# Expert loop of a hybrid block: biases in a tile of their own, token numbers copied apart, another place for the small tiles, and sums read three tokens a partition

## The chip, the cores and the metric

The kernel runs on one core of a Trainium2 chip. The metric is the time of one execution on the device, in microseconds (us); the time of a kernel is the median of several executions. The core has five engines that work side by side and wait for each other through semaphores: TensorE (PE; the load of its weights is listed apart as PEld), VectorE (DVE), ScalarE (ACT), GpSimd (POOL) and SyncE (SP). Transfers are issued from queues of SyncE, ScalarE and GpSimd (SPq, ACTq, POOLq) and carried out by 16 DMA engines. A profile is one execution taken by the hardware profiler.

## What is computed

An image of 2 x 256 x 48 x 48 goes through two layers: a convolution and attention layer, then a state-space layer with a mixture of experts on 2 x 2304 = 4608 tokens of 256 channels. The change concerns the last stage alone, the mixture of experts, and the writing of the result:

```python
def _L1_ffn_ref(x, Wg, bg, W1, b1, W2, b2):            # 8 experts, 256 -> 1024 -> 256
    gate_logits = xf @ Wg + bg
    top_w, top_i = jax.lax.top_k(gate_logits, 2)        # each token goes to two experts
    top_w = jax.nn.softmax(top_w, axis=-1)
    w_dense = jnp.sum(jax.nn.one_hot(top_i, E) * top_w[..., None], axis=1)
    for e in range(E):
        h = jax.nn.gelu(xf @ W1[e] + b1[e], approximate=False)
        out = out + w_dense[:, e:e + 1] * (h @ W2[e] + b2[e])
# ...
t = t + _L1_ffn_ref(_ln_t(t), ...)
x = _from_tokens(t, x)                                  # tokens x channels -> channels x tokens
```

## The kernel before

Before the expert stage every token has been written twice into a table in HBM (`xs`), once for each of its two experts, so that the rows of one expert stand together. A row has 256 channels, 8 gate weights and the number of the token (`XW` = 265 words). The residual stream stands in `acc`, one row of 256 channels a token. The expert stage works through 40 tiles: 36 of 256 rows ("pairs", the 2 in `tiles`) and 4 of 128 rows (the 1). Which rows and which expert a tile has is computed on the chip (`plan`). A branch for four more tiles of 128 rows stands behind the loop and is not taken here.

```python
every = NPAIR // (NUSUAL + 1)                     # 36 // 5 = 7: a 128-row tile after 7, 14, 21, 28 pairs
for i in range(NPAIR):
    tiles.append((2, i))
    if i % every == every - 1 and i // every < NUSUAL:
        tiles.append((1, i // every))
# ...
def fetch(i):                                     # rows and weights of tile i, issued by SyncE
    halves, n = tiles[i]
    x = hp.tile([P, 2, XW], F32, tag="ex", name="ex", bufs=4)[:, :halves]
    # ... (tile 0 apart)
    row = self.value(at[0:1, 0, n : n + 1], sp, NROWS - TR)
    part = self.value(at[0:1, 1, n : n + 1], sp, (E - 1) * P)
    nc.sync.dma_start(x, self.expert_rows(self.xs[bass.ds(row, halves * P), :]))
    wt = ew.tile([P, WCOL], F32, tag="wt", name="wt")               # 3 buffers: W1, W2, b1, b2, one-hot of the expert
    self.tc.keep_in_program_order(nc.sync.dma_start(wt, ins["We"][bass.ds(part, P), :]))
    fetched[i] = x, wt

def turn(i):                                      # rows transposed to ext; the gate weight of each row
    x, wt = fetched[i]
    xt = hp.tile([P, NH, halves * P], F32, tag="ext", name="ext")
    self.transposes(xt..., [x[:, j, k * P : (k + 1) * P] for k in range(NH) for j in range(halves)], nc.vector.tensor_copy)
    own = hp.tile([P, halves, E], F32, tag="own", name="own")
    nc.vector.tensor_tensor(own, x[:, :, C : C + E], bcast(wt[:, WCOL - E :], 1, [P, halves, E]), ALU.mult)
    weight = hp.tile([P, halves], F32, tag="weight", name="weight")
    nc.vector.tensor_reduce(weight, own, AX.X, ALU.add)

def weight_sums(i):                               # pairs: four sums of blocks of W2 (ts), VectorE
    # ... t1 = b12 - b11; t3 = b22 - b12; t2 = b22 - t1; t4 = b21 - t2
def hidden_sums(i):                               # pairs: four sums of blocks of hid (ss), VectorE
    # ... s3 = a11 - a21; s1 = a21 + a22; s2 = s1 - a11; s4 = a12 - s2

def up(i):                                        # hid = gelu(x W1 + b1)
    for c in range(NHC):                          # 8 times
        ps = self.bank()                          # 4 banks
        # ... two matmuls
        nc.scalar.activation(hid[:, c, :], ps[:, :rows], AF.Gelu, bias=b1[:, c : c + 1])

def finish(i, y, j):                              # weighted, and added to acc by an accumulating indirect DMA
    x, weight = fetched[i][0], turned[i][1]
    nc.scalar.activation(y, y, AF.Identity, scale=weight[:, j : j + 1])
    token = x[:, j, XW - 1 :].bitcast(I32)
    put = nc.gpsimd.indirect_dma_start(self.acc, bass.IndirectOffsetOnAxis(ap=token, axis=0), y, None, compute_op=ALU.add)
    # ... the two stores of one tile have no order between them; those of different tiles have

def down(i):                                      # y = hid W2 + b2
    # 128 rows: 8 matmuls, y = po + b2, finish
    # pairs: Strassen-Winograd's seven products of half size, four matmuls each, in the order
    #   a11 b11, s3 t3, a12 b21, a22 t4, s1 t1, s2 t2, s4 b22
    nc.scalar.copy(p1, p[1])
    # ... seven additions on VectorE make y0 and y1
    for j, y in enumerate((y0, y1)):
        add(y, y, b2)                             # b2 lies in wt
        finish(i, y, j)

def run(first, end):
    for i in range(first, end):
        up(i)
        if i + 1 < end: turn(i + 1)
        if tiles[i][0] == 2: hidden_sums(i)
        down(i)
        if i + 1 < end: weight_sums(i + 1)
        if i + 3 < end: fetch(i + 3)
# ...
for g in range(B * NBLK):                         # at the end: 12 blocks of 384 tokens of acc are read
    # ... a partition gets three tokens that lie 128 apart
    (nc.sync, nc.scalar)[g % 2].dma_start(t, self.acc[g * TB : (g + 1) * TB, :].rearrange("(j p) c -> p j c", p=P))
for g, t in enumerate(blocks):                    # transposed and written
    for k in range(NH):
        o = hp.tile([P, TB], F32, tag="o", name="o", bufs=6)
        self.transposes(o, [t[:, j, k * P : (k + 1) * P] for j in range(NJ)], nc.vector.tensor_copy)
        (nc.sync, nc.scalar)[k].dma_start(self.out[b, k * P : (k + 1) * P, blk * TB : (blk + 1) * TB], o)
```

The order of the instructions on each engine isn't that of this text: a scheduler moves instructions whose inputs are there ahead of others. In the loop `own` of a tile stands up to two tiles ahead of its place.

Of the kernel before, what the change touches and what calls it, by code (L numbers as in the profile page):

```python
# [31 lines left out]
F32 = mybir.dt.float32  # L32
I32 = mybir.dt.int32
AF = mybir.ActivationFunctionType
ALU = mybir.AluOpType
AX = mybir.AxisListType

P = 128
B, C, H, W = 2, 256, 48, 48
N = H * W  # L40
NH = C // P
# [23 lines left out]
NJ = 3  # L65
TB = NJ * P
NBLK = N // TB
# [3 lines left out]
E, HID = 8, 1024  # L71
NHC = HID // P
# [4 lines left out]
NPAIR, NSINGLE = 2 * B * N // TR, E  # L77
NUSUAL = E // 2
NROWS = E * PART + TR
XW = C + E + 1  # L80
WCOL = NH * HID + NHC * C + NHC + C + E
F32_EPS = float(np.finfo(np.float32).eps)


# [30 lines left out]
def bcast(ap, axis, shape):  # L115
    return ap.unsqueeze(axis).to_broadcast(shape)
# [108 lines left out]
class Kernel:  # L225
# [1496 lines left out]
    def experts(self, ctx):  # L1722
        nc, ins = self.nc, self.ins
        self.psum(ctx, 4, 2)
        hp = self.pool("eh", 2, ctx)
        ew = self.pool("ew", 3, ctx)
# [4 lines left out]
        fetched, turned, hidden, sums = {}, {}, {}, {}  # L1731

        tiles = []
        every = NPAIR // (NUSUAL + 1)
        for i in range(NPAIR):
            tiles.append((2, i))
            if i % every == every - 1 and i // every < NUSUAL:
                tiles.append((1, i // every))
        usual = len(tiles)
        tiles += [(1, i) for i in range(NUSUAL, NSINGLE)]  # L1740
# [10 lines left out]

        def fetch(i):
            halves, n = tiles[i]
            x = hp.tile([P, 2, XW], F32, tag="ex", name="ex", bufs=4)[:, :halves]
            if i == 0:
                self.tc.keep_in_program_order(nc.sync.dma_start(x, self.expert_rows(self.xs[0:TR, :])))
                fetched[i] = x, self.first_weights
                return
            at = where[2 - halves]
            row = self.value(at[0:1, 0, n : n + 1], sp, NROWS - TR)  # L1760
            part = self.value(at[0:1, 1, n : n + 1], sp, (E - 1) * P)
            nc.sync.dma_start(x, self.expert_rows(self.xs[bass.ds(row, halves * P), :]))
            wt = ew.tile([P, WCOL], F32, tag="wt", name="wt")
            self.tc.keep_in_program_order(nc.sync.dma_start(wt, ins["We"][bass.ds(part, P), :]))
            fetched[i] = x, wt

        def turn(i):

            halves = tiles[i][0]
            x, wt = fetched[i]  # L1770
            xt = hp.tile([P, NH, halves * P], F32, tag="ext", name="ext")
            self.transposes(
                xt.rearrange("p k q -> p (k q)"),
                [x[:, j, k * P : (k + 1) * P] for k in range(NH) for j in range(halves)], nc.vector.tensor_copy,
            )
            own = hp.tile([P, halves, E], F32, tag="own", name="own")
            nc.vector.tensor_tensor(  # L1777
                own, x[:, :, C : C + E], bcast(wt[:, WCOL - E :], 1, [P, halves, E]), ALU.mult
            )
            weight = hp.tile([P, halves], F32, tag="weight", name="weight")  # L1780
            nc.vector.tensor_reduce(weight, own, AX.X, ALU.add)
            turned[i] = xt, weight

        def weight_sums(i):

# [24 lines left out]

        def up(i):
            rows = tiles[i][0] * P
            xt, wt = turned[i][0], fetched[i][1]
            w1 = wt[:, : NH * HID].rearrange("p (k o) -> p k o", k=NH)
            b1 = wt[:, WCOL - C - NHC - E : WCOL - C - E]
            hid = hidden[i] = hp.tile([P, NHC, rows], F32, tag="hid", name="hid")
            for c in range(NHC):
                ps = self.bank()
                for k in range(NH):
                    nc.tensor.matmul(  # L1820
                        ps[:, :rows], lhsT=w1[:, k, c * P : (c + 1) * P], rhs=xt[:, k, :],
                        start=k == 0, stop=k == NH - 1,
                    )
                nc.scalar.activation(hid[:, c, :], ps[:, :rows], AF.Gelu, bias=b1[:, c : c + 1])  # L1824

        def finish(i, y, j):

            x, weight = fetched[i][0], turned[i][1]
            nc.scalar.activation(y, y, AF.Identity, scale=weight[:, j : j + 1])  # L1829
            token = x[:, j, XW - 1 :].bitcast(I32)  # L1830
            put = nc.gpsimd.indirect_dma_start(  # L1831
                self.acc, bass.IndirectOffsetOnAxis(ap=token, axis=0), y, None, compute_op=ALU.add
            )
            self.tc.declare_no_dep(put.ins, group=f"tile{i}", reason="a token has one row of an expert")
            self.tc.add_to_no_dep_group(f"tile{i}", put.ins)

        def down(i):
            wt, hid = fetched[i][1], hidden[i]
            w2 = wt[:, NH * HID : NH * HID + NHC * C].rearrange("p (k o) -> p k o", k=NHC)
            b2 = wt[:, WCOL - C - E : WCOL - E]  # L1840
            banks = self.ps2.tile([P, 2, 512], F32, tag="banks", name="po")
            if tiles[i][0] == 1:
                y = hp.tile([P, C], F32, tag="ey", name="ey", bufs=5)
                po = banks[:, 0, :C]
                for c in range(NHC):
                    nc.tensor.matmul(po, lhsT=hid[:, c, :P], rhs=w2[:, c, :], start=c == 0, stop=c == NHC - 1)
                nc.vector.tensor_add(y, po, b2)
                finish(i, y, 0)
            else:
                v = sums.pop(i)  # L1850
                p = {}

                for n, (name, a, w) in enumerate((
                    (1, "a11", "b11"), (7, "s3", "t3"), (2, "a12", "b21"), (4, "a22", "t4"), (5, "s1", "t1"),
                    (6, "s2", "t2"), (3, "s4", "b22"),
                )):
                    p[name] = banks[:, n // 4, n % 4 * P : (n % 4 + 1) * P]
                    for c in range(NHC // 2):
                        nc.tensor.matmul(p[name], lhsT=v[a][:, c], rhs=v[w][:, c], start=c == 0, stop=c == NHC // 2 - 1)  # L1859
                y0, y1 = (hp.tile([P, C], F32, tag="ey", name="ey", bufs=5) for _ in range(2))  # L1860
                p1, u2, u3, u4 = (hp.tile([P, P], F32, tag=f"u{j}", name=f"u{j}", bufs=1) for j in range(4))
                add = nc.vector.tensor_add
                nc.scalar.copy(p1, p[1])  # L1863
                add(y0[:, :P], p[2], p1)
                add(u2, p[6], p1)
                add(u3, p[7], u2)
                add(u4, p[5], u2)
                add(y1[:, :P], p[4], u3)
                add(y1[:, P:], p[5], u3)
                add(y0[:, P:], p[3], u4)  # L1870
                for j, y in enumerate((y0, y1)):
                    add(y, y, b2)
                    finish(i, y, j)
            del fetched[i], turned[i], hidden[i]
# [26 lines left out]
        with self.tc.If(self.value(many[0:1, 0:1], list(self.nc.engines), NSINGLE) > NUSUAL):  # L1901
# [2 lines left out]
            turn(usual)  # L1904
            run(usual, len(tiles))

        blocks = []
        for g in range(B * NBLK):
            b, blk = divmod(g, NBLK)
            t = self.x[b].rearrange("p k n -> p (k n)")[:, blk * NJ * C : (blk + 1) * NJ * C]  # L1910
            t = t.rearrange("p (j c) -> p j c", j=NJ)
            (nc.sync, nc.scalar)[g % 2].dma_start(
                t, self.acc[g * TB : (g + 1) * TB, :].rearrange("(j p) c -> p j c", p=P)
            )
            blocks.append(t)
        for g, t in enumerate(blocks):
            b, blk = divmod(g, NBLK)
            for k in range(NH):
                o = hp.tile([P, TB], F32, tag="o", name="o", bufs=6)
                self.transposes(o, [t[:, j, k * P : (k + 1) * P] for j in range(NJ)], nc.vector.tensor_copy)  # L1920
                (nc.sync, nc.scalar)[k].dma_start(self.out[b, k * P : (k + 1) * P, blk * TB : (blk + 1) * TB], o)

    def run(self):
        nc = self.nc
# [4 lines left out]
        for b in range(B):  # L1929
            for i in range(NX):  # L1930
                part = slice(i * N // NX, (i + 1) * N // NX)
# [25 lines left out]
        nc.vector.tensor_copy(self.taken, self.c["base"])  # L1957
        self.first_weights = self.pool("ew0", 1).tile([P, WCOL], F32, name="wt")
        nc.sync.dma_start(self.first_weights, self.ins["We"][0:P, :])
        with ExitStack() as l1:  # L1960
            self.mamba(l1)
        with ExitStack() as ffn:
            self.experts(ffn)


@with_exitstack
# [30 lines left out]
def _arrays(i):  # L1997
# [29 lines left out]
        "W_in": w_in, "W_out": at("W_out").T,  # L2027
        "We": experts.reshape(E * P, WCOL),
        "vec": np.concatenate([vec[k] for k in _VEC], axis=1),
# [21 lines left out]
```

## Time and profile before

| | |
|---|---|
| time | 1411.49 us, median of 3 (1408.32 to 1415.42) |
| span of the profile | 1414.2 us |
| TensorE busy | 1269.9 us, 90% |
| VectorE busy | 1013.5 us, 72% |
| ScalarE busy | 780.4 us, 55% |
| GpSimd busy | 531.3 us, 38% |
| the expert loop on TensorE | 838.4 to 1374.2 us, mean clock 0.99, 203 GB/s |
| from its end to the first read of the sums | 1374.2 to 1383.1 us |
| reading, transposing, writing | 1383.1 to 1414.2 us, 304 GB/s |

How to read lines of the profile. A line of the timeline gives the start and the length in us, the engine, the line of the kernel, the operation, what it writes and reads, how often, and in brackets how long the engine stood idle before it and what ended that. A line of the chain of work that ended last gives start, length and what it was. A line of the waits says who waited for whom, for how many us in all, how many times, and the longest. A stretch of the windows gives its length, the busy time of PE, PEld, DVE, ACT and POOL, the granted clock of TensorE as a share of full speed, the busy share of the DMA engines, and GB/s. `acc<-ey,ex` is the accumulating store of `finish`.

### The profile page before, as it was taken

How to read it: one execution, taken by the hardware profiler on the slowest of the kernel's cores; microseconds unless marked ns; L12 is line 12 of the kernel's file. 1: busy time of each engine (PE TensorE's matmuls, PEld its weight loads, DVE VectorE, ACT ScalarE, POOL GpSimd, SP SyncE). 2: the span in 40 equal slices, each digit the busy share in tenths (PEclk: the TensorE clock that was granted, in tenths of full speed). 3: DMA queues.
4: the chain of work that ended last, by engine and by line, in shares of the span. 5: the costliest groups of instructions: out<-in, count | busy, mean ns of one | idle time of the engine just before them, and what ended most of it. 6: DMA issues, size and time to landing. Idle time of an engine off the chain costs nothing.

```text
span 1414.2 us, 23686 instructions
## 1 busy us (share of the span) xinstructions
PE 1269.9 (90%) x8144; PEld 1012.9 (72%) x8144; DVE 1013.5 (72%) x2610; ACT 780.4 (55%) x1920; POOL 531.3 (38%) x648
## 2 busy tenths in 40 slices
PE   5999999998998899999988539998999999999983
PEld 4566767666666566666665429997998999998983
DVE  4999999997788889899978636654645645655653
ACT  2688877897987777777866212332332332432320
POOL 5213030111466777778676831221222222221220
PEclk9999999997999999999999859999999999999996
DMA  7321413121332233324243147666566667666628
GB/s 285 107 88 46 138 38 105 37 64 65 116 99 82 68 90 107 101 93 120 82 127 100 57 134 279 209 194 214 177 217 225 180 218 232 196 208 219 203 50 275
DMA packets 100442, 199.54 MB, mean 141 GB/s; under 512 B 10059, under 2 KB 86044, under 8 KB 94876
## 3 DMA queue, kind: packets, MB, share of 16 engines
q1 hardware_dynamic: 80540, 171.57, 36.4%
q0 software_dynamic: 14400, 19.74, 6.6%
q10 hardware_dynamic: 5380, 6.69, 1.4%
q8 instruction: 66, 1.08, 0.3%
q14 instruction: 56, 0.46, 0.1%
HBM read 158.71 MB, written 44.18 MB: 143 GB/s over the span
## 4 chain that ended last, share of the span: by engine, by line
PE 38%; DVE 15%; DMA 14%; ACT 3%; issue 3%; POOL 2%; another core or an unknown queue 0%; SPq 0%; DVEq 0%; ACTq 0%; POOLq 0%
PE bank L1820 11%; PE po L1859 10%; DMA wt<-in_We 7%; DMA acc<-ey,ex 5%; PE bank L909 4%; PE zbank L909 3%; PE bank L1420 2%; DVE xc L1106 2%; PE bank L895 1%; PE bank L1359 1%; PE bank L1402 1%; DVE mt L1322 1%; ACT mt L1314 1%; DVE y L1410 1%; POOL xs L1629 1%
## 5 line engine op out<-in xcount | busy, mean ns | idle before, releaser
L1820 PE MATMUL bank<-ext,wt 128*128 128x256 f32 (+1 forms) x1280 | 275.5, 373 | 10.0 <-ACT hid L1824 9.2
L1831 POOL DMA_INDIRECT acc<-ey,ex x76 | 118.5, 1559 | 435.0 <-ACT ey L1829 394.8
L1820 PEld LDWEIGHTS bank<-ext,wt 128*128 128x128 f32 x1280 | 233.0, 192 | 41.7 <-ACT hid L1824 11.7
L1824 ACT ACTIVATE hid<-bank,wt 128x256 f32<-128x256 f32 (+1 forms) x320 | 143.0, 462 | 83.0 <-PE bank L1820 79.0
L1863 ACT COPY u<-po 128x128 f32<-128x128 f32 x36 | 9.6, 266 | 226.6 <-PE po L1859 226.6
L1859 PE MATMUL po<-ts,ss 128*128 128x128 f32 x864 | 108.4, 275 | 0.0
L1859 PEld LDWEIGHTS po<-ts,ss 128*128 128x128 f32 x864 | 102.6, 192 | 0.0
L585 DVE SCALAR_TENSOR_TENSOR x<-hid,w2r,x 128x1128 f32<-128x1128 f32 (+3 forms) x72 | 99.9, 1392 | 0.4 <-ACT hid L579 0.2
L909 PE MATMUL bank<-xn,win 128*128 128x387 f32 x240 | 94.3, 517 | 1.1 <-DVE lg L1445 1.0
L1777 DVE TENSOR_TENSOR own<-ex,wt 128x16 f32<-128x16 f32 (+1 forms) x40 | 6.9, 173 | 122.9 <-DMA wt<-in_We 114.8
L674 POOL COPY kp<-kp 128x10 f32<-128x10 f32 (+1 forms) x60 | 23.4, 390 | 190.2 <-DVE kp L667 190.2
L793 ACT ACTIVATE prob<-prob,top 128x308 f32<-128x308 f32 x144 | 78.2, 549 | 17.4 <-DVE top L782 17.0
L1314 ACT ACTIVATE mt<-mt,cum 128x128 f32<-128x128 f32 x288 | 87.4, 392 | 0.0
L1106 DVE SCALAR_TENSOR_TENSOR xc<-bank,vec,xc 128x384 f32<-128x384 f32 x144 | 85.1, 605 | 2.4 <-ACT xc L1095 2.2
L909 PE MATMUL zbank<-xn,win 128*128 128x384 f32 x192 | 77.6, 529 | 4.2 <-ACT z L1216 4.2
L1629 POOL DMA_INDIRECT xs<-u,rows x72 | 71.9, 999 | 22.5 <-issue 16.7
L1859 PE MATMUL po<-wt,hid 128*128 128x128 f32 x576 | 77.5, 278 | 0.0
L1420 PE MATMUL bank<-wout,y 128*128 128x264 f32 x288 | 72.9, 398 | 2.6 <-DVE ss L1435 1.3
L1859 PEld LDWEIGHTS po<-wt,hid 128*128 128x128 f32 x576 | 71.7, 195 | 0.1
L824 PE MATMUL bank<-pt,val 110*64 110x128 f32 (+1 forms) x864 | 69.4, 278 | 0.8 <-ACT pt L814 0.8
L799 ACT ACTIVATE prob<-prob,rden 128x308 f32<-128x308 f32 x144 | 67.7, 547 | 4.3 <-DVE rden L848 4.2
L824 PEld LDWEIGHTS bank<-pt,val 110*64 110x64 f32 (+1 forms) x864 | 58.7, 136 | 14.7 <-issue 10.2
(288 smaller groups left out, 2982.7 us busy)
## 6 DMA issues: line engine op xcount, KB each, us to landing
wt<-in_We SPq DMA_DIRECT2D x40, 2184.0 KB
mt<-decays SPq DMA_DIRECT2D x36, 512.0 KB
ex<-xs SPq DMA_DIRECT2D x36, 265.0 KB
rd<-decays SPq DMA_DIRECT2D x68, 128.0 KB
val<-vtab SPq DMA_DIRECT2D x72, 110.0 KB
vraster<-vout SPq DMA_DIRECT2D x18, 256.0 KB
acc<-x SPq DMA_DIRECT2D x36, 128.0 KB
vtab<-vraster SPq DMA_DIRECT2D x12, 304.0 KB
```

What stands on the lines that cost most here:

```text
L585: nc.vector.scalar_tensor_tensor(dst, src, w[:, k : k + 1], dst, ALU.mult, ALU.add)
L793: nc.scalar.activation(t, t, AF.Exp, bias=T["top", c][:, a : a + 1], scale=-1.0, accum_out=T["den", c][:, a : a + 1])
L824: nc.tensor.matmul(po[j * HD : (j + 1) * HD, :P], lhsT=T["val", c][:nk, i, a * HD : (a + 1) * HD], rhs=T["pt", key][:nk, j, i, :], start=i ...
L909: self.nc.tensor.matmul(ps, lhsT=lhs(k), rhs=rhs(k), start=k == 0, stop=k == NH - 1)
L1106: nc.vector.scalar_tensor_tensor(out(), T["bank", ("cv", at)][:, i : i + TB], wc[:, i : i + 1], out(), ALU.mult, ALU.add)
L1314: nc.scalar.activation(t, t, AF.Relu, bias=at_s, scale=-1.0)
L1420: nc.tensor.matmul(ps[:, : C + E], lhsT=T["y", c][:, m, :], rhs=self.l1["wout"][:, m, :], start=m == 0, stop=m == NZ - 1,)
L1629: ins = nc.gpsimd.indirect_dma_start(self.xs, bass.IndirectOffsetOnAxis(ap=of("rows")[:, i, q : q + 1], axis=0), T["u2", g][:, i, :], None,)
L1820: nc.tensor.matmul(ps[:, :rows], lhsT=w1[:, k, c * P : (c + 1) * P], rhs=xt[:, k, :], start=k == 0, stop=k == NH - 1,)
L1824: nc.scalar.activation(hid[:, c, :], ps[:, :rows], AF.Gelu, bias=b1[:, c : c + 1])
L1831: put = nc.gpsimd.indirect_dma_start(self.acc, bass.IndirectOffsetOnAxis(ap=token, axis=0), y, None, compute_op=ALU.add)
L1859: nc.tensor.matmul(p[name], lhsT=v[a][:, c], rhs=v[w][:, c], start=c == 0, stop=c == NHC // 2 - 1)
```

## The change

It has four parts. The biases and the one-hot row leave the weight tile `wt` for a small tile `bt` with four buffers and a load of its own, so that a weight buffer is free when its matrices have been used and what needs only biases doesn't wait for the matrices. The token numbers are copied from the rows to a tile of their own, `token`, with three buffers, so that the rows (`ex`, three buffers in place of four) are free once they are turned. The 128-row tiles stand after each nine pairs, so that one of them is last. At the end a partition reads three neighbouring tokens in one piece of 3072 bytes, the transposed blocks are put in order by the copies out of PSUM, which VectorE and ScalarE share, and two blocks are written at a time.

```diff
-        every = NPAIR // (NUSUAL + 1)
+        every = NPAIR // NUSUAL
...
-            x = hp.tile([P, 2, XW], F32, tag="ex", name="ex", bufs=4)[:, :halves]
+            x = hp.tile([P, 2, XW], F32, tag="ex", name="ex", bufs=3)[:, :halves]
...
-            wt = ew.tile([P, WCOL], F32, tag="wt", name="wt")
-            self.tc.keep_in_program_order(nc.sync.dma_start(wt, ins["We"][bass.ds(part, P), :]))
-            fetched[i] = x, wt
+            bt = hp.tile([P, WCOL - WMAT], F32, tag="bt", name="bt", bufs=4)
+            self.tc.keep_in_program_order(nc.sync.dma_start(bt, ins["We"][bass.ds(part, P), WMAT:]))
+            wt = ew.tile([P, WMAT], F32, tag="wt", name="wt")
+            self.tc.keep_in_program_order(nc.sync.dma_start(wt, ins["We"][bass.ds(part, P), :WMAT]))
+            fetched[i] = x, wt, bt
...
-                own, x[:, :, C : C + E], bcast(wt[:, WCOL - E :], 1, [P, halves, E]), ALU.mult
+                own, x[:, :, C : C + E], bcast(bt[:, NHC + C :], 1, [P, halves, E]), ALU.mult
...
+            token = hp.tile([P, halves], I32, tag="token", name="token", bufs=3)
+            nc.vector.tensor_copy(token, x[:, :, XW - 1].bitcast(I32))
...
-            token = x[:, j, XW - 1 :].bitcast(I32)
             put = nc.gpsimd.indirect_dma_start(
-                self.acc, bass.IndirectOffsetOnAxis(ap=token, axis=0), y, None, compute_op=ALU.add
+                self.acc, bass.IndirectOffsetOnAxis(ap=token[:, j : j + 1], axis=0), y, None, compute_op=ALU.add
             )
...
-                t, self.acc[g * TB : (g + 1) * TB, :].rearrange("(j p) c -> p j c", p=P)
+                t, self.acc[g * TB : (g + 1) * TB, :].rearrange("(p j) c -> p j c", j=NJ)
...
-                o = hp.tile([P, TB], F32, tag="o", name="o", bufs=6)
-                self.transposes(o, [t[:, j, k * P : (k + 1) * P] for j in range(NJ)], nc.vector.tensor_copy)
-                (nc.sync, nc.scalar)[k].dma_start(self.out[b, k * P : (k + 1) * P, blk * TB : (blk + 1) * TB], o)
+                o = op.tile([P, 2, TB], F32, tag="o", name="o")            # 6 buffers, a pool of its own
+                for i in range(2):
+                    ps = self.bank()
+                    for j in range(NJ):
+                        nc.tensor.transpose(
+                            ps[:, j * P : (j + 1) * P], blocks[g + i][:, j, k * P : (k + 1) * P], self.ident
+                        )
+                    (nc.vector.tensor_copy, nc.scalar.copy)[i](
+                        o[:, i].rearrange("c (p j) -> c j p", j=NJ), ps[:, :TB].rearrange("c (j p) -> c j p", j=NJ)
+                    )
+                (nc.sync, nc.scalar)[k].dma_start(self.out[b, k * P : (k + 1) * P, blk * TB : (blk + 2) * TB], o)
```

Where the biases are used (`up`, `down`), `wt` becomes `bt`; the last part stands in a method of its own (`results`) with its own pools.

## The prediction

> **What bounds the kernel now.** I read the busy shares first, then the chain of work that ended last in order of time, then the waits, and the timeline of one tile at last.
>
> The page gives TensorE 90% of the span. From 838 us on the kernel is the expert loop, one tile after the other: 36 tiles of 256 rows and 4 of 128. The timeline of TensorE has each 256-row tile begin 13.60 us after the one before (1347.22 to 1360.82) and a 128-row tile take 7.47 us (936.50 to 943.97). So the loop is at least 36 x 13.60 + 4 x 7.47 = 519.5 us, and it lasts from 838.43 to 1374.15 = 535.7 us. The loss is 16.2 us: tile 0 at a low clock took 16.26, and the tile two places behind each 128-row tile lost 7.3, 3.9, 1.3 and 1.6 us (20.93, 17.46, 14.87 and 15.21 us in place of 13.60). The chain shows the first (start, length, what):
>
> ```profile
> 952.27 0.55 DVE ext L897
> 952.82 10.53 DMA wt<-in_We
> 963.57 0.57 issue
> 964.14 0.68 DVE ts L1794
> ```
>
> and the waits of the whole loop (who waited for whom: us in total, times, the longest), of the DMA queue of SyncE and of the engines:
>
> ```profile
> SPq L1762 <- DMA acc<-ey,ex: 331.1, 41, 17.5
> ```
>
> ```profile
> DVE own L1777 <- DMA wt<-in_We: 114.8, 34, 9.2
> ```
>
> To be seen: VectorE stood 9.2 us at `own` for a weight load issued at 952.82. It was issued so late because the queue first waited for an accumulating store to land before it could refill `ex` (SyncE waited 331.1 us for these in all). Elsewhere the 114.8 us of waiting at `own` ends just in time and costs nothing.
>
> The end: the last matmul ends at 1374.15, the sums are read from 1383.11 on, the last 27 us move 9.4 MB.
>
> ```profile
> 1383.11 6.76 SPq L1912 DMA_DIRECT2D x<-acc  x6
> ...
> 1401.01 9.36 DVE L897 COPY o<-bank 128x384 f32<-128x384 f32 x18 [8.91 <-DMA out<-o]
> ```
>
> A store that nothing disturbs lands 1383.11 - 1380.70 = 2.4 us after GpSimd ends it (the last one of the fence on GpSimd further down ends at 1379.15 + 1.55). VectorE waited 8.9 us for a free `o`, so the writes ran in two bursts.
>
> **What the Trainium skill says.** "DMA: Bandwidth & Descriptors", section "Queues, rings and completion order": each DMA engine goes round the queues that have work, a packet at a time. The trace agrees in effect: in the lines below a store ended by GpSimd at 1250.25 lands only at about 1256.6 (the queue's next step), 6.4 us later, because a weight load was issued at 1246.41; that one landed at about 1255.7. "TensorE: Matmul & The Clock Gate", opening table: the queues of VectorE and ScalarE are strict FIFOs. The 9.2 us at `own` agree: work behind it that was ready stood too. "DMA: Bandwidth & Descriptors", section "Why small descriptors are slow (HBM only)": each packet carries a fixed overhead. The trace agrees: the input with rows of 3072 bytes came at 416 GB/s, the sums in pieces of 1024 bytes at 350 GB/s, the engines full in both (the two stretches below end with the DMA engines' share and GB/s).
>
> ```profile
> 4.00:6.00 2.00, 0.00 (x0) 0.00 (x0) 0.94 (x3) 0.00 (x0) 0.00 (x0) 1.00 1.04 416
> ...
> 1390.00:1392.00 2.00, 2.00 (x12) 2.00 (x11) 1.75 (x4) 0.00 (x0) 0.00 (x0) 0.50 1.10 350
> ```
>
> ```profile
> 1246.41 0.33 SPq L1764 DMA_DIRECT2D wt<-in_We  x1
> 1256.72 0.38 SPq L1762 DMA_DIRECT2D ex<-xs  x1
> ```
>
> ```profile
> 1248.69 1.56 POOL L1831 DMA_INDIRECT acc<-ey,ex  x1 [0.30 <-issue]
> ```
>
> **The change, part by part.**
>
> *Loads earlier.* `ex` is free once its tile is turned, no longer after its store has landed; `wt` is free at the last matmul of `down`, no longer after the bias addition about 3.3 us later. `own` needs only the small `bt`. So a weight load starts about 0.45 us after the tile's last matmul and has over a tile to spare. The losses behind 128-row tiles for this reason go: -14.1 us.
>
> *The token copy: a new wait.* The copy has three buffers, and a store reads its buffer until it has landed. The build of the changed kernel shows where it stands on VectorE: `ss` (s3), token copy, `ss` (s1), `ext`, `ss` (s2), `ss` (s4). The copy is that of the tile two ahead, and it waits for both stores of the tile just before, on the semaphores of these very stores. VectorE works in order, so s1, `ext`, s2 and s4 of every tile now stand behind the landing of the last tile's stores. I take times from the start D of a tile on TensorE (1347.22, 1360.82) from the timeline, of VectorE in the tile of 1347.22, of TensorE in its last three products, and of GpSimd:
>
> ```profile
> 1354.84 0.69 DVE L1806 TENSOR_TENSOR ss<-hid 128x512 f32<-128x512 f32 x1 [1.06 <-ACT hid L1824]
> 1355.45 0.68 DVE L897 COPY ext<-bank 128x512 f32<-128x512 f32 x1
> 1356.05 0.68 DVE L1807 TENSOR_TENSOR ss<-ss,hid 128x512 f32<-128x512 f32 x1
> 1356.77 0.69 DVE L1808 TENSOR_TENSOR ss<-hid,ss 128x512 f32<-128x512 f32 x1
> ```
>
> ```profile
> 1358.14 1.95 PE L1859 MATMUL po<-ts,ss 128*128 128x128 f32 x16
> 1359.93 1.06 PE L1859 MATMUL po<-wt,ss 128*128 128x128 f32 x8
> ```
>
> ```profile
> 1364.76 1.56 POOL L1831 DMA_INDIRECT acc<-ey,ex  x1 [8.78 <-ACT ey L1829]
> 1366.62 1.55 POOL L1831 DMA_INDIRECT acc<-ey,ex  x1 [0.30 <-issue]
> 1377.29 1.56 POOL L1831 DMA_INDIRECT acc<-ey,ex  x1 [9.11 <-ACT ey L1829]
> 1379.15 1.55 POOL L1831 DMA_INDIRECT acc<-ey,ex  x1 [0.30 <-issue]
> ```
>
> The second store of the tile before is ended by GpSimd at D + 7.35 (1368.17, with D = 1360.82). Undisturbed it lands at D + 7.35 + 2.4 = D + 9.75. But the weight load now runs from D + 0.45, its data from about D + 2.2 (in the trace 1.8 us after the issue) for some 4.7 us, then `ex` and `bt` for about 1.4, and the two stores need 1.4 us of the DMA engines each (1381.0 to 1382.5 in the quiet case). That is 8.9 us of work from D + 2.2, so the engines are full until about D + 10.5, and I put the landing L at D + 11.1 (estimate from these rows; 10.2 to 12 possible). Then s1 is ready at L + 0.85, s2 (behind s1 and `ext`, 1.2 us later) at L + 2.06. The sixth of the seven products needs s2 and with the seventh takes 1.79, so the next tile starts at L + 3.85, and about 0.2 more for weight loads that can no longer be hidden: D + 15.1, against 13.6. Loss: 1.5 us for each of 31 tiles = +46 us. The threshold is L = D + 9.6: earlier it costs nothing, later it costs in full.
>
> *Behind the three 128-row tiles inside the loop* VectorE's addition of that tile's bias also stands behind a token copy (about 3.7 us late), with the Gelus of the next tile behind it on ScalarE, and that next tile's s3 behind the store of the 128-row tile: I estimate 2.6 us each, +8 us.
>
> *A 128-row tile last.* One store after the last matmul in place of two. Its start is bound by the landing of the last pair's second store: pair ended + 7.35 + 2.4, then 1.56 + 2.4 = 13.7 us, less the 7.1 us of the small tile = about 6.5 us after the last matmul, where it was 9.0: -2.5 us.
>
> *The sums.* 4.72 MB read in pieces of 3072 bytes: 13.4 us at 350 GB/s become 11.4 at 416: -2. Written in pieces of 3072 for 1536 bytes (360 GB/s before): about -1.5. Twice as much of `o` in flight, so the trough at 1400 to 1404 (260 and 286 GB/s) fills: -1. Copies shared by two engines are then no limit. Together -4.5 us.
>
> Sum: -14 + 46 + 8 - 2.5 - 4.5 = +33; since the landing enters 34 times and its likelier errors are towards the quiet case, I take +28: 1440 us.
>
> **Rivals.** (1) The wait is hidden: the stores land before D + 9.6. For it: the weight load now starts 3 us earlier and is nearly done when the second store begins. Against it: `ex` and `bt` follow at once, and the quiet landing is already D + 9.75. Time: 1411 - 21 = about 1390. (2) The stores stay behind all that SyncE's queue moves, as at 1256.6, where landing came 0.9 us after the weights': L = D + 12, 2.4 us a tile, about 1470. (3) The DMA becomes the bound, with 3 issues a tile: 8.9 us of work in 13.6, so no. (4) TensorE falls to a low clock: its gaps stay near 1.5 us, where 4.7 us of standing gave a clock of 0.84 in that tile; little.
>
> **Range and chances.** 0.5 us in L is 17 us in the end. L from 10.0 to 12.0 gives roughly 1400 to 1472: this is my range of 8 in 10. The line of 2% slower is 1439.7, so slower and same are about even: 0.5 and 0.48. Faster by over 2% (under 1383) needs no stall at all and more than I can find at the end: 0.02.
>
> **What would show it.** In the waits of VectorE: the token copy waiting for the stores, 3 to 5 us a tile, more than 100 us in all, and TensorE idle in `po` waiting for `ss`, some 1.5 us a tile; a period of TensorE of about 15.1 us. `own` waiting for nothing, SyncE no longer for stores. The last read at 400 GB/s or more. I am wrong if tiles still follow each other at 13.6 us: then the time is near 1390; or if they do not, but another wait stands ahead of the token copy.

## The result, and the profile after

| | before | after |
|---|---|---|
| time, median of 4 runs each | 1409.90 us (1406.99 to 1415.42) | 1458.28 us (1455.23 to 1464.87) |
| ratio | | 1.0345, 95% interval 1.0296 to 1.0393 |
| span of the profile | 1414.2 us | 1456.6 us |
| first to last matmul of the expert loop | 535.7 us | 583.2 us |
| last matmul to first read of the sums | 9.0 us | 7.5 us |
| first read of the sums to the end | 31.1 us | 28.3 us |

The changed kernel is 3.4% slower. The whole loss lies in the expert loop, 47.5 us; the two stages behind it gained 4.3 us. (The profile of before was taken at the upper end of its times, so the spans differ by less than the medians.)

The waits of the expert loop in the changed kernel come first. A line has who waited for whom, us in total, how many times, the longest.

```profile
DVE token L1788 <- DMA acc<-ey,token: 218.6, 37, 10.5
...
PEld po L1864 <- DVE ss L1813: 27.6, 29, 1.9
...
PE bank L1826 <- ACT hid L1830: 16.8, 3, 5.8
```

The token copy on VectorE waited in 37 of its 40 times for the stores of an earlier tile to land. Two waits of TensorE follow from it: one of up to 1.9 us in 29 tiles, for a sum of `hid` that stands behind the copy, and one of up to 5.8 us that occurs three times only. `own` waits for nothing any more, and SyncE's longest wait is now for TensorE to finish with a weight buffer, no longer for stores:

```profile
SPq L1769 <- PE po L1864: 365.1, 33, 12.8
```

The chain of work that ended last shows one ordinary tile (start, length, what). The tile started on TensorE at D = 1311.07:

```profile
1316.56 0.30 issue
1316.86 5.75 DMA acc<-ey,token
...
1322.70 0.17 DVE token L1788
1322.87 0.60 DVE ss L1813
1323.47 0.04 issue
1323.52 1.16 PE po L1864 x8
1324.68 0.04 issue
1324.72 2.05 PE po L1864 x16
1326.77 1.30 PE bank L1826 x6
```

Read from the top: GpSimd begins the second store of the tile before, it lands at about 1322.6 (D + 11.6), the copy of 0.17 us goes, then the sum s1, and only then three of the seven products of this tile. The next tile starts at 1326.61, 3.9 us after the copy began and 15.54 us after D, in place of 13.60. It is so in all of the 29 ordinary pairs that were compared: the copy begins between D + 10.1 and D + 11.7, D + 10.94 in the mean, and the next tile starts 3.9 us later each time.

Behind a 128-row tile inside the loop it is worse. The timeline there (start, length, engine, line, operation; in brackets how long the engine stood idle and what ended that):

```profile
980.03 3.62 PE L1826 MATMUL bank<-ext,wt 128*128 128x256 f32 x16
...
987.88 0.17 DVE L1788 COPY token<-ex 128x2 int32<-128x2 int32 x1 [10.42 <-DMA acc<-ey,token]
987.96 0.42 DVE L1852 TENSOR_TENSOR ey<-po,bt 128x256 f32<-128x256 f32 x1
988.41 0.51 ACT L1835 ACTIVATE ey<-ey,weight 128x256 f32<-128x256 f32 x1 [11.29 <-DVE ey L1852]
...
989.33 5.80 PE L1826 MATMUL bank<-ext,wt 128*128 128x256 f32 x16 [5.69 <-ACT hid L1830]
```

The 128-row tile's last matmul had ended at about 980.2, but its bias addition stood behind the copy until 987.96. The scaling on ScalarE stood behind the addition, the next tile's Gelus behind the scaling, and TensorE, its four banks full, stood for 5.69 us. When it went on, 16 matmuls took 5.80 us where the 16 before the stop took 3.62 us. (The trace has two records for each matmul of the text, so x16 is half of a pair's first stage.) The stretches of that tile (length, busy time of PE, PEld, DVE, ACT, POOL, then the granted clock, the DMA engines' share, GB/s) show TensorE at a standstill and then busy at half its clock:

```profile
984.00:986.00 2.00, 0.00 (x0) 0.00 (x0) 0.00 (x0) 0.00 (x0) 0.00 (x0) 1.00 1.01 390
...
990.00:992.00 2.00, 2.00 (x6) 1.61 (x5) 0.00 (x0) 0.84 (x3) 0.75 (x1) 0.50 0.49 80
```

That tile took 21.63 us.

Summed over the loop, from the starts of the tiles: 30 ordinary pairs lost 37.5 us (1.25 each, 0.4 to 2.0), the three pairs behind a 128-row tile 8.0, 7.1 and 7.9 us (23.0), tile 0 1.0 us more than before; the old losses of 14.1 us are gone. 37.5 + 23.0 + 1.0 - 14.1 = 47.4 us, which is the loop's 47.5.

The reading of the sums now runs at 404 to 415 GB/s (350 before), but with six `o` the last stage still has a hole; the stretches of it:

```profile
1434.00:1436.00 2.00, 2.00 (x10) 1.70 (x8) 1.18 (x2) 0.57 (x2) 0.00 (x0) 0.50 1.03 415
...
1440.00:1442.00 2.00, 0.74 (x7) 0.50 (x5) 0.00 (x0) 0.00 (x0) 0.00 (x0) 1.00 0.98 229
```

### The profile page after: what moved, and what is told of

It is laid out like the page before. It is cut to its first block, busy times and chain, and to the rows that moved or that the text cites. A ratio compares the mean times of both kernels' runs of the same rounds, so it can differ in the third digit from the quotient of the medians.

```text
span 1456.6 us, 23803 instructions
## 1 busy us (share of the span) xinstructions
PE 1287.0 (88%) x8144; PEld 1017.2 (70%) x8144; DVE 1009.3 (69%) x2638; ACT 787.3 (54%) x1932; POOL 531.3 (36%) x648
## 4 chain that ended last, share of the span: by engine, by line
PE 34%; DMA 15%; DVE 13%; POOL 5%; issue 4%; ACT 4%; SPq 0%; another core or an unknown queue 0%; DVEq 0%; ACTq 0%; POOLq 0%
DMA acc<-ey,token 11%; PE po L1864 9%; PE bank L1826 9%; PE bank L910 4%; POOL acc L1836 3%; PE bank L1421 2%; PE zbank L910 2%; DMA ex<-xs 2%; DVE xc L1107 1%; PE bank L1403 1%; PE bank L1360 1%; DVE ss L1813 1%; DMA cz<-bc 1%; POOL xs L1630 1%; ACT ey L1835 1%
## 5 line engine op out<-in xcount | busy, mean ns | idle before, releaser
L1826 PE MATMUL bank<-ext,wt 128*128 128x256 f32 (+1 forms) x1280 | 278.9, 377 | 18.1 <-ACT hid L1830 16.8
L1836 POOL DMA_INDIRECT acc<-ey,token x76 | 118.3, 1557 | 481.9 <-ACT ey L1835 467.0
L1826 PEld LDWEIGHTS bank<-ext,wt 128*128 128x128 f32 x1280 | 236.6, 195 | 50.2 <-ACT hid L1830 18.0
L1830 ACT ACTIVATE hid<-bank,bt 128x256 f32<-128x256 f32 (+1 forms) x312 | 141.5, 460 | 91.8 <-PE bank L1826 86.4
L1788 DVE COPY token<-ex 128x2 int32<-128x2 int32 (+1 forms) x40 | 6.7, 167 | 218.6 <-DMA acc<-ey,token 218.6
L1864 PE MATMUL po<-ts,ss 128*128 128x128 f32 x864 | 118.4, 282 | 23.2 <-DVE ss L1813 22.0
L1864 PEld LDWEIGHTS po<-ts,ss 128*128 128x128 f32 x864 | 104.1, 191 | 33.9 <-DVE ss L1813 27.6
```

The source lines that it names most:

```text
L1826: nc.tensor.matmul(ps[:, :rows], lhsT=w1[:, k, c * P : (c + 1) * P], rhs=xt[:, k, :], start=k == 0, stop=k == NH - 1,)
```

## The experiments

Theory: the copy is cheap and its wait unavoidable with so few buffers, but it stands in VectorE's queue ahead of work that TensorE needs, and the stores that it waits for land late because of the weight loads. Rivals: the new order and number of loads is what costs; or three buffers are too few whoever copies. The columns: the loop from first to last matmul, the stage from the first read of the sums to the end, both from the profile of one execution; the ratio is to the kernel before, measured beside it. That kernel's median moved between 1408.58 and 1412.13 us from one set of runs to the next, so small differences are to be read from the ratios and not from the column of times.

| run | loop us | stage us | time us | ratio, 95% interval |
|---|---|---|---|---|
| before | 535.7 | 31.1 | 1409.90 | 1 |
| changed | 583.2 | 28.3 | 1458.28 | 1.0345 (1.0296 to 1.0393) |
| changed, four token buffers | 524.8 | 28.2 | 1393.11 | 0.9907 (0.9875 to 0.9940) |
| changed, copy on GpSimd | 522.4 | 27.6 | 1395.98 | 0.9879 (0.9839 to 0.9920) |
| changed, weights not loaded | 529.9 | 29.1 | 1399.90 | 0.9946 (0.9930 to 0.9962) |
| changed, three loads left out | 600.6 | 27.8 | 1474.51 | 1.0459 (1.0416 to 1.0501) |
| changed, no token copy | 536.1 | 27.1 | 1404.16 | 0.9982 (0.9966 to 0.9998) |
| the same, three `bt`, twelve `o` | 524.2 | 27.1 | 1393.00 | 0.9870 (0.9838 to 0.9901) |
| before + split of biases | 524.2 | 30.6 | 1401.21 | 0.9929 (0.9907 to 0.9951) |
| before + 128-row tile last | 532.7 | 31.2 | 1407.77 | 0.9981 (0.9966 to 0.9997) |
| before + new reading and writing | 536.7 | 27.1 | 1406.31 | 0.9995 (0.9976 to 1.0014) |
| four token buffers, twelve `o` | 524.0 | 27.1 | 1396.01 | 0.9884 (0.9854 to 0.9915) |
| copy on GpSimd, twelve `o` | 524.8 | 27.0 | 1391.71 | 0.9871 (0.9837 to 0.9905) |

**Four token buffers.**

```diff
-            token = hp.tile([P, halves], I32, tag="token", name="token", bufs=3)
+            token = hp.tile([P, halves], I32, tag="token", name="token", bufs=4)
```

> The changed kernel with four buffers for the token numbers in place of three; nothing else. On VectorE the copy now stands behind the last of the four hidden sums (s4), where nothing urgent follows it, and still waits for stores. Theory (the wait at the copy holds up the sums behind it): pairs follow each other at 13.6 us again, TensorE no longer waits for ss, and the loop falls from 583 to about 525 us: about 1398 us, some 60 less than the changed kernel and 1% less than before. Rival (the new order of loads and the third issue per tile are the cost, the wait at the copy only shows it): the period stays near 15 us and the time within 1% of 1458 us.

Measured 1393.11 us, 65 us less than the changed kernel. Pairs take 13.60 us again, those behind 128-row tiles 13.89, 14.37 and 14.61. In the timeline of VectorE the copy now stands behind s4 (L1815) and `own`, and still ends a wait for a store:

```profile
1317.65 0.69 DVE L1815 TENSOR_TENSOR ss<-hid,ss 128x512 f32<-128x512 f32 x1
...
1319.12 0.15 DVE L1788 COPY token<-ex 128x1 int32<-128x1 int32 x1 [0.71 <-DMA acc<-ey,token]
```

The copies waited 44.0 us in the whole loop, at places where nothing was urgent. One more buffer didn't take the wait away: it let the scheduler place the copy a tile further ahead, and that place is a harmless one.

**The copy on GpSimd, with three buffers.** Is it then the number of buffers or the place?

```diff
-            nc.vector.tensor_copy(token, x[:, :, XW - 1].bitcast(I32))
+            nc.gpsimd.tensor_copy(token, x[:, :, XW - 1].bitcast(I32))
```

> The changed kernel with its three token buffers, but the copy done by GpSimd in place of VectorE. It waits for the same two stores as now, and stands right ahead of the next tile's stores on GpSimd, which has been idle some 10 us a tile there. Theory (it is the place of the wait in VectorE's queue that costs, not the wait): pairs at 13.6 us, no TensorE wait for ss, about 1392 to 1396 us, as with four buffers on VectorE. Rival (three buffers are too few: whoever copies must wait for the stores, and the chain copy, store, landing sets the period): 15 us a pair, about 1455 us.

Measured 1395.98 us, and a loop without any loss behind its first two tiles: the pairs take 13.60 us, the three behind 128-row tiles too. A copy and the store after it in the timeline of GpSimd; the tile there began at 1298.90:

```profile
1309.97 0.19 POOL L1788 COPY token<-ex 128x2 int32<-128x2 int32 x1 [3.26 <-DMA acc<-ey,token]
1316.91 1.55 POOL L1836 DMA_INDIRECT acc<-ey,token  x1 [6.74 <-ACT ey L1835]
```

The landing is as late as ever, at D + 11.1, the copy waits 3.26 us for it, and GpSimd then stands another 6.74 us for ScalarE. The same buffers, a wait for the same stores (91.4 us in the loop), and no cost: it is the place. Both rivals fall.

**Weights not loaded.** Why does the landing come at D + 11 and not at the quiet D + 9.75?

```diff
+            if i > 1:
+                fetched[i] = x, self.kept, bt
+                return
-            wt = ew.tile([P, WMAT], F32, tag="wt", name="wt")
+            wt = ew.tile([P, WMAT], F32, tag="wt", name="wt", bufs=1)
             self.tc.keep_in_program_order(nc.sync.dma_start(wt, ins["We"][bass.ds(part, P), :WMAT]))
+            self.kept = wt
```

> The changed kernel with the copy and its three buffers, but the matrices are loaded for the second tile only and kept; this leaves out 38 weight loads of about 2 MB (a wrong result, the same instructions otherwise). Theory (the stores land late, at D + 11.6 us, because they share the DMA engines with the weight load): they land at about D + 9.8, the copy still waits (about 1 to 2 us less of it each tile, the threshold being D + 9.6), pairs follow at 13.6 to 13.9 us, about 1400 to 1408 us. Rival (the landing depends on GpSimd and the store alone): D + 11.6 and 15.1 us as now, about 1455 us.

Measured 1399.90 us (38 weight loads are left out). In the timeline, the start of a tile and the copy in it:

```profile
1300.37 7.07 PE L1830 MATMUL bank<-ext,wt 128*128 128x256 f32 x32
...
1310.06 0.17 DVE L1792 COPY token<-ex 128x2 int32<-128x2 int32 x1 [3.88 <-DMA acc<-ey,token]
```

The copy goes at D + 9.69, in the next tile at D + 9.64, and these tiles take 13.59 and 13.61 us. Here VectorE still stands 3.88 us for the store, 141.3 us in the whole loop, in the same place as in the changed kernel, and it costs little (529.9 us of loop), because the copy begins at D + 9.80 in the mean, near the threshold of D + 9.6. That is 1.1 us earlier than in the changed kernel, and there all of this delay is paid. Two things moved in this run, though: the load of the rows, which stood right behind that of the weights (`ex` issued at D + 1.4 in the tile shown above), is issued at D + 7.5 here. What each of the two does by itself was not separated. The packets of the changed kernel show the order: in 30 ordinary pairs those of the weights run from D + 1.2 to between D + 7.3 and D + 8.7, and of the bytes of the two stores 5% have moved by D + 8.0 and 95% by D + 9.8 (medians), though GpSimd had ended the first store at D + 5.5. The stores come mostly behind the weights.

**Three loads left out behind the 128-row tiles.**

```diff
+            if i > 3 and tiles[i - 3][0] == 1:
+                fetched[i] = x, fetched[i - 1][1], bt
+                return
             wt = ew.tile([P, WMAT], F32, tag="wt", name="wt")
```

> The changed kernel without the weight loads that SyncE issues at the end of the three 128-row tiles inside the loop (the tile three places on uses the matrices of the tile before it; 3 of 39 loads are left out, a wrong result). Theory (the stores of the pair ahead of a 128-row tile land 7.9 us after GpSimd ended them, at 987.8 for 979.9, because this load's packets come with theirs, and the addition of the 128-row tile's bias, its scaling and the next Gelus stand behind that landing): the stores land 3 us later at most, the tile behind a 128-row tile takes 13.6 to 16 us in place of 20.7 to 21.6, some 17 to 22 us less in all, 1436 to 1441 us. Rival (the chain of waits behind a 128-row tile costs this by its order, whatever is loaded): 20 us or more still, 1453 us or more.

Measured 1474.51 us, 16 us more than the changed kernel: the expectation failed. The timeline behind the first 128-row tile:

```profile
983.82 0.17 DVE L1791 COPY token<-ex 128x2 int32<-128x2 int32 x1 [7.78 <-DMA acc<-ey,token]
...
985.00 0.33 SPq L1772 DMA_DIRECT2D wt<-in_We  x1
985.13 1.56 POOL L1839 DMA_INDIRECT acc<-ey,token  x1 [6.66 <-ACT ey L1838]
985.27 6.65 PE L1829 MATMUL bank<-ext,wt 128*128 128x256 f32 x16 [3.05 <-ACT hid L1833]
...
993.59 0.17 DVE L1791 COPY token<-ex 128x2 int32<-128x2 int32 x1 [8.42 <-DMA acc<-ey,token]
```

The first landing did come earlier, as the theory had it: 5.3 us after GpSimd ended the store (at 978.47) in place of 8.0, and TensorE stood 3.05 us in place of 5.69. But its clock still fell (0.50 from 984.4 to 991.2, 16 matmuls in 6.65 us), and the next weight load was issued at 985.00, right ahead of the 128-row tile's own store, which so landed only at about 993.5, 6.8 us after its end; in the changed kernel no weight load was on the way then, and it took 2.2 us. The copy that waits for it stands ahead of s3. The three tiles behind 128-row tiles lost 25.0 us (23.0), and the three after those 22.2 us (4.4). A load taken from one place brought the next one to a worse place, so the time of this run doesn't tell what the load that was left out had cost. Taking one transfer away doesn't cure the wait; taking all of them away nearly does, and moving the copy does.

**No token copy.** The other way to undo it: the store reads the number from the rows, and `ex` has its four buffers.

```diff
-            token = hp.tile([P, halves], I32, tag="token", name="token", bufs=3)
-            nc.vector.tensor_copy(token, x[:, :, XW - 1].bitcast(I32))
...
-            x = hp.tile([P, 2, XW], F32, tag="ex", name="ex", bufs=3)[:, :halves]
+            x = hp.tile([P, 2, XW], F32, tag="ex", name="ex", bufs=4)[:, :halves]
...
-                self.acc, bass.IndirectOffsetOnAxis(ap=token[:, j : j + 1], axis=0), y, None, compute_op=ALU.add
+                self.acc, bass.IndirectOffsetOnAxis(ap=token, axis=0), y, None, compute_op=ALU.add
```

> The changed kernel without the token copy: the store reads the token number from the rows again, and ex has four buffers again, as before; the split of biases and matrices, the 128-row tile at the end and the new way of reading and writing the sums stay. Theory (the copy's wait is the cost): about 1398 to 1402 us, the same as with four token buffers; SyncE waits for stores again, a few hundred us in all, at no cost, since own needs only the small bt. Rival (the split is the cost: three loads a tile, or weights landing at a worse time): stays over 1440 us.

Measured 1404.16 us: 54 us of the loss go, but the loop keeps 11 us over that with four token buffers. The waits of the loop name it:

```profile
DVE own L1782 <- DMA bt<-in_We: 151.7, 34, 7.6
```

"Own needs only the small `bt`" was half the truth: SyncE waits for a store before it refills `ex`, `bt` stands behind `ex` in its queue, and `own` behind `bt`. Behind the first 128-row tile VectorE stood 7.53 us, and the pair two places behind it took 18.94 us.

**The split alone, on the kernel before.** As in the change, but with three `bt`, and nothing else:

```diff
+            bt = hp.tile([P, WCOL - WMAT], F32, tag="bt", name="bt", bufs=3)
+            self.tc.keep_in_program_order(nc.sync.dma_start(bt, ins["We"][bass.ds(part, P), WMAT:]))
-            wt = ew.tile([P, WCOL], F32, tag="wt", name="wt")
-            self.tc.keep_in_program_order(nc.sync.dma_start(wt, ins["We"][bass.ds(part, P), :]))
+            wt = ew.tile([P, WMAT], F32, tag="wt", name="wt")
+            self.tc.keep_in_program_order(nc.sync.dma_start(wt, ins["We"][bass.ds(part, P), :WMAT]))
```

> The kernel before with the biases and the one-hot row in a small tile of their own (three buffers) and nothing else: the rows are still held until the stores have landed. The prediction's step (own needs only the small load, so the losses behind 128-row tiles go): about 14 us less, a ratio of 0.990. Rival, from the run without the token copy: SyncE still waits for a store ahead of ex, the small load stands behind ex in its queue, own waits for it up to 7.5 us and loses behind 128-row tiles nearly what it lost before: 0 to 4 us less, a ratio of 0.997 to 1.000.

Measured 1401.21 us, 10 us less than before (7 to 13 by the interval): nearer to the prediction's 14.1 than to the 0 to 4 of the rival that I had set against it. All pairs take 13.60 us but for 15.08 and 14.37 behind the first two 128-row tiles. Here too `own` waits for `bt`, but less:

```profile
DVE own L1780 <- DMA bt<-in_We: 43.9, 35, 6.3
```

The build shows the difference: with three `bt`, `own` stands on VectorE between s3 and s1; with four, half a tile earlier, behind s4 and ahead of `ts`.

**Three `bt` without the copy, twelve `o`.** That tests it:

```diff
-            bt = hp.tile([P, WCOL - WMAT], F32, tag="bt", name="bt", bufs=4)
+            bt = hp.tile([P, WCOL - WMAT], F32, tag="bt", name="bt", bufs=3)
...
-        op = self.pool("o", 6, ctx)
+        op = self.pool("o", 12, ctx)
```

> No token copy at all (the store reads the number from the rows, ex with four buffers), the split with three instead of four buffers of bt, a 128-row tile last, twelve o. In the build own now stands between the hidden sums s3 and s1 of a later tile, half a tile later on VectorE than with four buffers of bt, where it stood ahead of ts. Theory (where a wait stands on VectorE decides, and with bt three deep own comes after its small load has landed): the 10 us that the run without the copy lost against four token buffers go, pairs at 13.6 us also behind 128-row tiles, about 1394 to 1397 us, a ratio of 0.988 to 0.990. Rival (that loss comes from 128-row tiles after nine pairs and the loads they delay): about 1402 us, a ratio of 0.995 to 0.997.

Measured 1393.00 us; the loop is 524.2 in place of 536.1 us, and `own` waited 36.7 us in all in place of 151.7. One buffer fewer made the loop 12 us faster. With three buffers the loads of `bt`, and of `wt` behind it, also wait for the bias addition and so go later; how much of the 12 us is the place and how much the later loads wasn't separated.

**The two other parts, on the kernel before.** The last tile:

```diff
-        every = NPAIR // (NUSUAL + 1)
+        every = NPAIR // NUSUAL
...
-            if i % every == every - 1 and i // every < NUSUAL:
+            if i % every == every - 1:
```

> The kernel before with the 128-row tiles after each nine pairs, one of them last; nothing else. Theory: three tiles in place of four inside the loop lose as the tile two behind a 128-row tile does (7.3, 3.9, 1.3, 1.6 us before, 3.5 on average), 3 to 4 us less, and the end from the last matmul to the first read of the sums falls by 1.4 us as it did in the changed kernel: together 4 to 5 us less, a ratio of 0.997. Rival (the loss behind a 128-row tile depends on where the transfers stand, and the first is the worst wherever it is): 1 to 2 us less.

Measured 1407.77 us, 2.7 us less (0.4 to 4.8). In its profile the loop is 3.0 us shorter and the time to the first read 7.4 us, where it was 9.0. The losses behind the three 128-row tiles are 4.8, 1.5 (0.9 more two tiles on) and 4.0 us, 11.2 us in place of 14.1: fewer such tiles, and the first is the worst again.

The new reading and writing is the whole of `results` put into the kernel before:

```diff
-                t, self.acc[g * TB : (g + 1) * TB, :].rearrange("(j p) c -> p j c", p=P)
+                t, self.acc[g * TB : (g + 1) * TB, :].rearrange("(p j) c -> p j c", j=NJ)
... (and the copies and writes of two blocks, as in the change)
```

> The kernel before with the new way of reading and writing the sums alone (three tokens a partition, two blocks written at a time, copies shared by VectorE and ScalarE). From the changed kernel's trace, where this stage took 26.9 us in place of 29.2: 2 to 3 us less than before, a ratio of 0.998. Prediction's figure: 4.5 us less (ratio 0.997). Rival (the end is bound by bytes alone): no difference.

Measured a ratio of 0.9995 (0.9976 to 1.0014): by the times alone not told from nothing. The profiles are clearer: from the first read of the sums to the end the three kernels with the old code took 31.1, 31.2 and 30.6 us, the seven with the new one and six `o` 27.1 to 29.1, mean 27.9: 3 us less.

**Twelve `o`.** On the kernel with four token buffers, and on that with the copy on GpSimd:

```diff
-        op = self.pool("o", 6, ctx)
+        op = self.pool("o", 12, ctx)
```

> The kernel with four token buffers and twelve instead of six buffers of o in the last stage. Theory (the last stage still stands in the changed kernel's trace at 1440 to 1442, with 227 and 230 GB/s, because all six o are being written): the trough fills, 2 us less than with six, a ratio to before of 0.989 and the lowest time of all. Rival (read and write share the DMA engines, which are full on average): the same as with four token buffers, 1393 us.

> The changed kernel with its three token buffers, the copy on GpSimd, and twelve o. If the two gains add up (the loop at its least time with the copy on GpSimd, a fuller last stage with twelve o): a ratio to before of 0.986 to 0.988, 1392 to 1394 us, 1 to 2 us under the run with six o. If the last stage is bound by its bytes: 0.988, as with six.

Measured ratios of 0.9884 (0.9854 to 0.9915) and 0.9871 (0.9837 to 0.9905). Against their pairs with six, 0.9907 and 0.9879, these can't be told apart. In the profiles the stage took 27.1, 27.0 and, without the copy, 27.1 us: 0.8 us under the mean with six. So the hole is worth about 1 us at most, not 2; a difference of 0.8 lies within the spread of 27.1 to 29.1 that the six-buffer profiles have. All five kernels whose loop runs at its full pace lie between 0.987 and 0.991 and beat both kernels; the fourth token buffer or the copy on GpSimd, each an edit of one line of the changed kernel, gets there.

## Why the prediction was right, and where its sizes were off

It said slower about as likely as same, 1440 us within 1400 to 1472; it is slower, 1458.28. The mechanism that it named is the one that the runs show. The terms as measured below add up to 42 us, where the working had 33: one was 8.5 us too large and another 15 us too small, so that the total came nearer than its parts. The terms:

- *Loads earlier, -14.1.* Right. With the copy on GpSimd no loss behind a 128-row tile is left, and the split alone shortened the loop by 11.5 us and the time by 10. Its reason needs an addition: `own` still waits for a load behind a store unless the rows are free early or `own` stands late enough.
- *The token copy, +46.* Right in mechanism, and the mean a little high: 1.25 us for each of 30 pairs, 37.5 us. The chain from landing to next tile, put at 3.85 and 0.2 us, measured 3.9 from the start of the copy. The threshold D + 9.6 is borne out by the run without weight loads (copy at D + 9.69 and D + 9.64, no loss). The landing was put at D + 11.1; the copy began at D + 10.94 in the mean and never after D + 11.7, so rival (2), D + 12, was too late and rival (1) too early.
- *How that landing was worked out.* The figure is partly luck. The working has the DMA engines full until D + 10.5 and the landing 0.6 us later, although its own sum, 2.2 + 8.9, gives 11.1. In the tile shown the engines' share falls from 0.65 to 0.08 at 1321, D + 9.9, and the landing comes 1.6 us after that; the two errors cancel. The Trainium skill, in "DMA: Bandwidth & Descriptors", section "Queues, rings and completion order", has each DMA engine go round the queues that have work, a packet at a time. The packets here show little of that: of the 0.26 MB of the stores in that tile 0.01 MB had moved by 1319, and 0.15 MB moved in the next us, when the loads were ending. In that rival (2) was right, which had the stores behind the weights; but the weights were through by D + 8.7.
- *Behind the three 128-row tiles, +8.* This is the term that was mis-sized: 23.0 us. Two things in it. The bias addition was put 3.7 us late; it came 7.7 us late (987.96 for 980.2). Of this 2.6 us go with another weight load, issued at 980.22, just as the store ended at 979.9: with that load left out the addition came 5.1 us late (983.90 for 978.8); where the other 1.4 us come from stays open. And rival (4), a low clock, was dismissed because gaps would stay near 1.5 us. They do in ordinary tiles, but this gap was 5.69 us, and then 16 matmuls took 5.80 in place of 3.62 us. 5.69 + 2.18 = 7.87 us, nearly the whole 8.0 of that tile. The Trainium skill has it in "TensorE: Matmul & The Clock Gate", section "Part 1: The HAM clock gate (the "warmup" mystery)": half rate after an idle window of about 3.4 us. The three stops of over 3.4 us in the loop of the changed kernel (5.69, 5.33 and 5.78) agree, and so do the ordinary ones of up to 1.7 us, which left the clock at 1.00. In between the runs go both ways, and shorter stops were enough: see the last section.
- *A 128-row tile last, -2.5.* -1.5 us (7.5 for 9.0); alone in the kernel before, -1.6 (7.4).
- *The sums, -4.5.* -2.8 in this pair of profiles, 3 in the mean. The trough did not fill with six double buffers: the copies stopped for 5.1 us for want of an `o`.
- *Taken +28 for +33.* The allowance for a quieter landing went the right way for the pairs, and the term behind the 128-row tiles took more than it gave.

## What to carry to other kernels

An instruction that waits for a buffer to come free is paid by everything behind it on its in-order engine, so look in the build where it stands and not only how long it waits: the wait for the same stores cost 61 us (583.2 for 522.4 us of loop) with the loop's urgent sums behind it and nothing on an engine that had time. In these builds the number of buffers moved the place where the scheduler put an instruction; one more (`token`) took a wait out of the way, and one fewer (`bt`) went with a loop 12 us shorter. When a wait is estimated, ask also whether TensorE will stand for several us in one piece: the slow matmuls that followed such a stop cost another 2 to 3 us here.

## What the runs showed of the hardware beyond that

- After 5.69 us without a matmul TensorE ran at a clock of 0.50 until 993.6, though it was busy from 989.33 on: 16 matmuls took 5.80 us. After 3.05 us in the run with three loads left out they took 6.65 us, 3 us more than the 3.62 at full clock: a shorter stop cost more.
- The length of a stop alone doesn't tell what follows. In the loops of the runs every stop of 3.4 us or more was followed by a halved clock, and none under 1.9 us. In between it went both ways: 3.09 us in the run without the token copy left the clock at 1.00, and 1.93 us in the kernel before halved it. The same four matmuls after each of these two stops:

```profile
1254.78 1.13 PE L1824 MATMUL bank<-ext,wt 128*128 128x256 f32 x4 [3.09 <-ACT hid L1828]
```

```profile
1075.47 1.83 PE L1820 MATMUL bank<-ext,wt 128*128 128x256 f32 x4 [1.93 <-ACT hid L1824]
```

- An accumulating store landed 2.2 to 2.4 us after GpSimd ended it when no weight load was on the way, 4.2 us in the ordinary tile shown, with a weight load ahead (1318.42 to 1322.61), and 6.8 to 7.9 us when the load was issued within 2 us of the store's end (979.9 to 987.8; 986.7 to 993.5).
